# Gates spread from SBUF instead of DRAM, the inputs loaded first, a longer clear behind each scatter, and a new order of the streams

## The chip, the cores and the metric

The kernel runs on one core of a Trainium2 chip. The metric is the device time of one execution in microseconds (us). Beside the timed runs there is one execution with a profile; its span is the time from the first to the last recorded instruction.

## The reference

Eight sequences of 512 tokens with 128 features pass through four residual blocks. All arithmetic is float32.

```python
x = embeddings                                   # (8, 512, 128)
x = x + causal_attention(layernorm(x), W_Q, W_K, W_V)
x = x + moe_ffn(layernorm(x), Wg, W1, W2, W3, Ws1, Ws2, Ws3)
x = x + rwkv_block(layernorm(x), ...)            # scan over time, channel mix of width 512
x = x + moe_ffn(layernorm(x), Wg, W1, W2, W3, Ws1, Ws2, Ws3)
```

`moe_ffn` softmaxes `x @ Wg` over 32 experts and keeps the 4 largest per token. Each expert has a capacity of 2048 pairs of token and expert. A chosen expert gives `silu(x @ W1[e]) * (x @ W3[e]) @ W2[e]` (128 to 64 to 128 features), weighted with the softmax score, and a shared expert of width 128 is added.

## The kernel before

All eight sequences stay in SBUF as residual tiles `res0` to `res7` (128 x 4 x 128). Work is written as Python generators, one for each step of the network and each sequence or group; a `yield` ends a piece. `ORDER` is a long string of two-character names, and `play` takes one piece of the named stream at each. This sets the order of the instructions on every engine (PE, DVE, ACT, POOL) and of the DMAs that SP issues. [...]

The names in `ORDER`: `a` is attention with the routing of the first expert layer, `r` the RWKV block with the routing of the second, `x` and `y` the shared expert of the first and second layer. The expert layers are done in two ways, by sequence (`RUNS`):

- Paged (sequences 1 to 3 and 4 to 6 in layer one, 0 to 2 and 3 to 5 in layer two). `scatter` (`s` in layer one, `t` in layer two; L506) writes each normalized token row to four places of a DRAM buffer `xs`, sorted by expert. One sequence is 16 indirect DMAs, issued by POOL, with a `pause()` behind each: a memset of the tile `idle`, 128 x `PAUSE` columns (L308), which nothing reads. `experts` (`k l m n`, in layer two `K L M N`) loads 512 rows at a time (`xg<-xs`, L554), 20 units for a group of three sequences, and stores the results (`ys<-oc`, L616). The first unit of a group waits for all 48 scatters of the group. `combine` (`u`, `v`; L657) adds the rows back with 16 indirect DMAs for each sequence.
- Full (sequences 0 and 7 in layer one, 6 and 7 in layer two). Every expert is computed for every token, two experts at a time, in 16 steps. `gates` makes a tile `gT` with one row of gate values for each expert (32 x 512) and stores it to a DRAM tile `gd` (L495). `full_up` (`d`, `D`) spreads rows 2i and 2i+1 of `gd` to 64 partitions each: one DMA of 256 KB into a tile `g` (L692), three steps ahead, in four buffers. Each step has two matmuls (L703), a tanh on ACT (L706), and on DVE the products L709, L710 (which reads `g`) and L711. `full_down` (`e`, `E`) multiplies by W2 and sums (L677).

SP issues nearly all transfers in the order in which the pieces are played: gate loads, expert loads and stores are in one queue. The tiles of most intermediate results come from the pool `work`, `NWORK` buffers of one shape each. `gT` and the transposed input `fT` of a full sequence are such tiles; `fT` is held until the last step of `full_up`.

At the start SP issues the `x` tiles of sequences 0 to 3, then the clearing of `xs0` (two DMAs of 2600 KB, L182), then the tiles of sequences 4 to 7, then the expert weights `pair`, `w2s` and `w13s`. The weights of the other blocks (`sm`) come on ACT's queue.

Of the kernel before, what the change touches and what calls it, by code (L numbers as in the profile page):

```python
# [9 lines left out]
F32 = mybir.dt.float32  # L10
# [59 lines left out]
for _name, _w in (  # L70
# [9 lines left out]


ORDER = (
    "a2a0a2a1a0a2a2a0a1a3z0a2a0a1a6a3z0a0a2a3a4a2a0a1a0a6a6a4a1a2a2a5a0z0a0a2a2a1a4a5a0a0a2a5a2a0a0a2"
    "a1a3a0a3a2a7a2a0a2a0a2a1a2a2a0a3a7a0a2a1a6a3a0a0a7a2a0a2a1a2a1a0a2a1a2a2a3a0a2a1a4a3a1a2a2a0a0a1"
    "a2a0a0a3a2a0a5a1a2a2a3a2a0a0a1a1a3a2a1a1a3a0a1a2a0a7a3a0a2a0a1a2a0a3a2a0a1a3a2a6a1a0a3a1a6a0a3a6"
    "a2a1a0a3a6a2a2a0a1a0a3a2a6a2a2a0a1a6a6a0a1a3a0a1a1a0a3a0a1a6a0a1a1a0a0a3a6a3a3a1a1a3a0a6a6a1a0a0"
    "a3a1a6a2a1a3a0a6a2a3a6a4a3a4a3a4a1a1a3a4a4a1a0a5a4a4a5a1a1a3a0a6a3a1a0a3a1a6a1a4a6a3a4a4a1a3a6a1"
    "a5a3a6a3a4d0a6a5a1a3a3a6a1a1a3a2a1a4a2a5a4a4a5d0a2a1d0a5a5a2a5x0x0a2a1a2s1a3a3a6x2a4a5a6x2x0x2x2"
    "a5a6a3a4a3x2x2a6s2a4a4d0a3x2a6a3a4a6a5x0a3a4a6a5a4s2a3a6a4x0a6a3a3a4a5d0a3d0s2x0a3a6x0a7a3a6l0a6"
    "a4a7s3l0a6l0a6a4a5d0a4a5a4x3a6a4a6x3d0s3a4d0a4a5d0a7a5a5a7a5a7a4a5a7d0a6a4a5x3s3a6a4a5a4x3a5a4a5"  # L90
    "x3a4a5x3a4a5s3a5x3a5a5a7a5e0a7a5a7e0a7a5d0a4e0a5d0a7e0s2a5a6a4a5d0a5d0a6a7a6e0d0a6a7a5a7x1a5s1d0"
    "a7x1x1a4a7e0a7a4d0a4d0a4a7a4a7a7x1s1a4d0d0a7d0e0d0a7a4x1s1d0d0d0a4a4d0a7e0a4e0x1k0a5d0a6a4a5a6x1"
    "d0a5d0k0a4a5k0e0a5d0s4k0l0k0x4l0l0a5d0x4d0a5l0s4d0m0a5e0m0l0a5d0d0e0l0l0l0s4m0a5m0k0k0k0l0k0d0a5"
    "n0s4n0l0a5d0l0l0d0n0m0d0n0e0m0k0l0k0a7s5n0l0l0l0l0n0a6a7l0l0x4l0k0a6m0k0k0a6e0s5k0m0m0x5m0l0a6x5"
    "n0d0n0d0n0l0l0x5s5a6x5l0n0a7x4a7a6k0l1m0k0x5l1m0x5d0s6l1l0x5x4n0l0l0l0l0n0k0l0l0m0l0k0a7m0k0l0a7"
    "k0s6m0l0l0n0l0m0a7n0k0l0a7k0m0l0l0n0l0m0x4n0s6a7k0x4l0k0m0l0l0n0l0m0a7n0n0a7k0l0n0s6k0m0l0l0a7l0"
    "m0k0l0a7k0a7m0n0m0x6n0l0s5l0n0l0x6l0n0k0l0l0m0x6x6k0l0m0e0k0l0x6k0a7m0l0l0n0l0m0x6n0a7a7k0l0k0m0"
    "l0n0l0l0a7m0l0n0a7k0x6l0m0k0k0n0k0l0a7l0m0l0n0a7k0a7m0k0n0m0n0n0l0a7l0l0n0k1l0a7a7m0a7l0l0a7m0n0"
    "l0l0n0k1l0l0m0l0a7k1m0k1l1a7k1m0l1l1n0l1m0x7n0l1x7m1x7k1l1l1l1n0k1x7n0m1m1k1x7m1l1k1n1l1l1l1l1n1"
    "u2k1m1l1l1l1k1n1m1x7n1m1l1x7m1k1l1l1n1l1k1e7n1l1u2m1l1l1k1l1n1m1k1d0n1d0m1k1d0m1n1k1l1n1n1l1l1d7"  # L100
    "l1l1u2n1k1m1l1l1l1k1e0m1k1m1l1k1m1n1l1l1l1l1n1k1m1l1l1l1k1n1u2m1k1m1n1l1m1k1n1l1l1d0l1n1d0m1d0k1"
    "m1n1k1l1n1n1u1l1l1l1l1n1k1m1l1l1l1k1e0m1k1m1r2e0l1m1k1n1r0d7n1r2d7n1l1l1l1r0n1k1m1r2k1r0u1r0d7l1"
    "m1r0l1n1r0d7e7l1r0l1n1r2u1m1k1r0r0m1k1l1d7r0r0d7r0l1l1l1l1r0u1n1r0m1k1n1l1r2e7r2r0r2r0r0r0r0r0m1"
    "u3r0l1n1k1d7r0n1r0r2k1d7r2k1r0k1r2r0u3r0r0l1r0m1r1m1n1r0l1n1k1r1l1l1l1r0m1r1r0r1u3r2r2d7r1l1r1e7"
    "l1r0r1r0m1u3r0d7r0l1r1r0r2l1d7r1r0r2r2r2r2r0r1m1r0r0r1r1d7r0r0m1r3r1l1r0r0l1r1r3l1n1r0l1r0r1n1r3"
    "r1r1r3m1r0r0m1r1r1r1r2r1n1r0r2r3d7r0e7r0r1n1n1r1d7n1r0r0r1r0r1r0u4r0r0r1r1r0r1r0r1r2r0r1r0u4r0r0"
    "r1r2r1r0y0r1r3t0r2r1r3r2y0r1r1r3r2r3r1t0r2r1r3r1r1r3r3r2r1r1d7r3r2r1t0r3r1r3r2y0d7r1r2r1r3r3d7t0"
    "r3d7r3e7r1r1r3r3r2d7r1r2u4r3r2r1e7r2d7r3y0r2r2r2r3r2r2r1r2r2r3u4r2r2r1r2r2r3r3r1d7r3r1r3r2d7r1u5"
    "d7r1y0r2d7r1r4d7r1d7e7r4r1r2d7r3r2u5r1r4r4r1r4r1d7r2e7d7e7r4r4r1r3r2r3u5r1y1r4r4d7y1r3r4r4d7y1r3"
    "d7r3r4r2d7y1u5r4r3r4r4r4r4d7r3r4r3y1r4r4y1r3r4d7r3y1u6e7r4r3r4r3e7r3r3r4y0r3r4r3y0r5u6r4r4r2r2r3"  # L110
    "d7r3r4r4r5r2r3d7r2r3r4d7r2u6e7r5r2r5r4r2r5r2r5d7d7r4r5r3r2r2d7r2u6r4r5e7r5r4r4r2r4r5r5r5r2r4L0r3"
    "r3d7t2r4L0d7r4L0r6r5r4d7r3r5r4r4d7d7r5r6r4r4t2r3r6e7r5r5r4r4r5r5r5r5r6r5r3t2r6r5e7r4r3r4d7r5r5t2"
    "y2r4r4y2r5r5r6r3r4r6r5t1r4r5r6r6r4r3d7r6r6r4r3r3e7r4r5r4e7t1r4r6r5r5r4r5r6r5r6r4r3r6t1r4r3r5r5r6"
    "r5r4r5r5r5t1r4r5r5r5r5r5r5r6r4r4r6t4y4r5r6r5r6y4K0r6r6r5r5K0t4K0K0K0L0r6L0L0L0L0K0M0L0L0L0M0N0t4"
    "K0r6M0N0K0L0M0N0K0r6N0L0L0L0L0t4K0M0L0L0L0M0N0K0r6M0N0K0L0M0r3N0K0L0L0r7y3N0r5r6y3r5t3r5L0L0y3M0"
    "L0L0K0y4M0r5L0K0N0r5r6y2M0N0K0r6t3r5M0L0K0N0r5r5y3N0y4r5L0L0L0r6y3M0K0r5r5t3M0L0K0N0y3N0r5y2y3r7"
    "r5L0r6r5y5L0r6L0L0t5K0M0L0K0L1r7M0L1y4N0L0L1y2r7L0L0r6K0L0N0M0t5r6r7r7r6r6M0r7K0L0t5L0N0r6r7K0N0"
    "M0L0K0M0r6L0L0N0L0r6L0N0M0t5L0L0K0L0r6M0N0K0L0r6M0N0L0K0M0r6N0L0L0K0t3N0L0r6M0L0K0r6M0N0L0L0K0N0"
    "L0r6M0L0K0r6M0L0L0K0y5y5N0r6M0N0L0M0K0L0N0L0L0K0r6N0M0L0r6M0r6K0N0K0K0N0L0r6r7L0L0K0L0r7r6r7r6M0"
    "K0L0r7M0N0L0L0K0L0N0r6r7L0M0L0K1r7y5M0L0y4r6r7N0r7r7M0y4L0N0y5M0r6L0N0L0L0r6K1r7y5N0K1r6r7M0L1y5"  # L120
    "M0K1N0L1L1r6L1K1N0r7M1L1r6r6M1N1r6r7K1N1v0y2L1L1r6K1L1L1y2r6L1L1r7M1L1r6K1y6M1N1K1r7y6M1L1M1v2N1"
    "N1L1L1y6K1L1N1y6K1L1D6y6M1L1L1K1r7y6M1K1L1L1y6N1L1L1r7v2M1N1K1E6M1N1L1K1L1N1M1r7K1M1r7K1L1L1L1L1"
    "r7N1v2L1L1r7M1N1K1M1L1N1K1L1N1M1L1L1K1M1L1N1K1M1L1N1M1r7N1L1L1L1v2K1N1D6K1r7D6M1D6r7K1L1M1N1L1L1"
    "L1K1D6N1D6v0M1K1D6M1r7N1K1L1N1r7D6L1L1r7v2D6r7L1K1D6r7M1r7v0M1L1K1r7N1L1L1D6L1N1K1M1K1r7M1E6r7L1"
    "v0N1D6L1L1D6r7N1E6r7r7L1L1r7M1L1K1M1r7L1L1K1v1M1L1v0r7M1N1L1L1L1K1N1N1K1L1N1M1L1L1K1L1r7v1M1K1M1"
    "L1r7M1r7N1K1N1N1L1L1L1K1K1D6N1r7K1D6M1r7v1r7E6D6E6L1M1N1L1L1L1L1N1r7M1L1L1L1E6M1N1r7M1D6v1N1M1D6"
    "N1D6r7N1r7D6r7D6E6D6r7v4D6r7r7v1r7D6r7E6D6r7r7y7y7D6y7v4D6D6y7E6D6y7D6D6y7E6y7v4D6D6D6E7E6D6D6D6"
# [15 lines left out]
def kernel(ctx: ExitStack, tc: tile.TileContext, x, small, vecs, w13, w2, out):  # L143
    nc = tc.nc
# [8 lines left out]
    dram = ctx.enter_context(tc.tile_pool(name="dram", bufs=1, space=bass.MemoryType.DRAM))  # L153
# [44 lines left out]
    for s in range(2):  # L200
        for i in range(2):
# [3 lines left out]
                in_=w2[i * H : (i + 1) * H],  # L205
# [477 lines left out]
    def full_up(f, b):  # L683

        n = f"{f}_{b}"
        _, gd, xT, _ = routed[f][b]
        loaded = {}

        def load(i):
            if i < NP:  # L690
                loaded[i] = full.tile([P, S], F32, tag="g", name=f"g_{n}_{i}", bufs=4)
                nc.sync.dma_start(  # L692
                    out=loaded[i], in_=gd[2 * i : 2 * i + 2].unsqueeze(1).to_broadcast([2, H, S])
                )

        for i in range(3):
# [317 lines left out]
```

## Time and profile before

| what | value |
|---|---|
| median of the two timed runs | 1059.47 us (1058.66 to 1060.27) |
| the profiled execution | 1047.35 us |
| its span | 1045.6 us |
| mean granted clock of PE | 0.896 |
| gate loads `g<-gd` | 64, of 256 KB each |
| scatters `xs<-xn,rows`, mean | 192, of 1019 ns |
| pauses, memset 128 x 192, mean | 192, of 287 ns |
| combines `res<-ys,rows`, mean | 192, of 1610 ns |

Durations below are from the profiled execution. In the groups, a line gives the source line, the engine, the operation and the tiles, then busy us and mean ns of one, then the idle time of the engine ahead of the group and who ended it. In a line of the table of windows stand the window, the busy time of PE, of PE's weight loads, of DVE, ACT and POOL with their instructions, the granted PE clock, the busy share of the 16 DMA engines, and GB/s. The chain is followed back from the last instruction: each piece is what released the next one.

### The profile page before, as it was taken

What the parts mean: (1) busy time and instruction counts of PE and PEld (TensorE: products, weight loads), DVE (VectorE), ACT (ScalarE), POOL (GpSimd) and SP (SyncE); (2) the same over time, 40 slices, a digit from 0 to 9 for tenths busy, and PEclk for the clock granted to TensorE, in tenths of its full rate; (3) what the DMA queues carried; (4) which work ended last, traced back from release to release, by engine and by line L of the source; (5) the groups of instructions that cost most, each with busy time, mean ns of one, the idle gap of its engine ahead of it and who ended that gap; (6) DMA issues with size and microseconds to landing.
All of it is one profiled execution on the core that took longest, in us unless ns stands there. A gap on an engine that the chain in (4) does not pass through costs nothing.

```text
span 1045.6 us, 14396 instructions
## 1 busy us (share of the span) xinstructions
PE 806.6 (77%) x4096; PEld 559.8 (54%) x4096; DVE 588.2 (56%) x2008; ACT 474.1 (45%) x1130; POOL 617.1 (59%) x682
## 2 busy tenths in 40 slices
PE   4488689777599668787889888786993989856664
PEld 2266356555498555453455545564783757534332
DVE  2457576655245436699779679662482445522332
ACT  4375243323276447473445555455672656201010
POOL 4200778555701828848888888878036685788500
PEclk9699999978799979898999898898996999977787
DMA  9990112333356655322233211543456566344311
GB/s 271 249 262 25 69 57 74 110 91 100 94 143 160 137 136 126 58 56 33 59 59 54 41 42 42 158 114 107 111 138 129 126 147 137 80 75 91 65 58 54
DMA packets 158892, 108.15 MB, mean 103 GB/s; under 512 B 17760, under 2 KB 147168, under 8 KB 158560
## 3 DMA queue, kind: packets, MB, share of 16 engines
q1 hardware_dynamic: 124592, 80.59, 28.8%
q0 software_dynamic: 33792, 25.39, 13.9%
q10 hardware_dynamic: 432, 1.27, 0.4%
q8 instruction: 35, 0.57, 0.2%
q14 instruction: 41, 0.34, 0.1%
HBM read 60.32 MB, written 46.89 MB: 103 GB/s over the span
## 4 chain that ended last, share of the span: by engine, by line
PE 17%; DMA 13%; POOL 11%; issue 8%; DVE 7%; ACT 2%; SPq 1%; POOLq 0%; ACTq 0%; DVEq 0%
DMA g<-gd 7%; POOL res L657 6%; DMA xg<-xs 4%; POOL xs L506 3%; PE o L609 3%; PE acl L576 3%; PE turn_x L346 1%; DMA res<-ys,rows 1%; PE kk L926 1%; PE fsum L677 1%; PE ac L703 1%; POOL idle L308 1%; PE kv L935 1%; PE acl L597 1%; DMA ys<-oc 1%
## 5 line engine op out<-in xcount | busy, mean ns | idle before, releaser
L657 POOL DMA_INDIRECT res<-ys,rows x192 | 309.2, 1610 | 123.7 <-DMA xg<-xs 57.8
L506 POOL DMA_INDIRECT xs<-xn,rows x192 | 195.7, 1019 | 83.1 <-issue 61.8
L703 PE MATMUL ac<-fT,pair 128*128 128x512 f32 x256 | 138.9, 670 | 13.1 <-DVE g L710 13.0
L706 ACT ACTIVATE fh<-ac 128x512 f32<-128x512 f32 x64 | 38.2, 596 | 162.3 <-PE ac L703 130.6
L677 PE MATMUL fsum<-w2s,fh 128*128 128x128 f32 x512 | 78.5, 305 | 39.3 <-DVE fh L711 38.9
L677 PEld LDWEIGHTS fsum<-w2s,fh 128*128 128x128 f32 x512 | 73.1, 216 | 64.7 <-DVE fh L711 52.1
L576 PE MATMUL acl<-w13s,xgTs 128*128 x640 | 94.5, 294 | 16.3 <-issue 6.1
L609 PE MATMUL o<-w2s,hz 128*128 x640 | 94.1, 292 | 15.2 <-ACT wt L585 5.8
L609 PEld LDWEIGHTS o<-w2s,hz 128*128 128x128 f32 x640 | 85.4, 203 | 28.6 <-issue 11.6
L576 PEld LDWEIGHTS acl<-w13s,xgTs 128*128 128x128 f32 x640 | 85.0, 205 | 27.4 <-issue 13.4
L710 DVE TENSOR_TENSOR g<-g,ac 128x512 f32<-128x512 f32 x64 | 43.7, 682 | 88.7 <-DMA g<-gd 88.7
L346 PE MATMUL turn_x<-ident,xg 128*128 128x128 f32 x320 | 52.8, 292 | 46.7 <-DMA xg<-xs 45.5
L703 PEld LDWEIGHTS ac<-fT,pair 128*128 128x128 f32 x256 | 50.1, 215 | 59.6 <-issue 41.2
L564 ACT COPY xgTs<-turn_x 128x512 f32<-128x512 f32 x80 | 46.7, 583 | 72.5 <-PE turn_x L346 52.8
L335 POOL TENSOR_TENSOR rstd_f<-rstd_f,nhalf 128x4 f32<-128x4 f32 x16 | 19.5, 1217 | 100.6 <-DVE wt L581 42.6
L581 DVE TENSOR_TENSOR wt<-acl,xg 128x4 f32<-128x4 f32 x80 | 12.8, 161 | 108.9 <-PE acl L576 74.6
L587 DVE SCALAR_TENSOR_TENSOR h<-h,acl 128x256 f32<-128x256 f32 x80 | 33.5, 418 | 68.0 <-ACT h L584 59.0
L346 PEld LDWEIGHTS turn_x<-ident,xg 128*128 128x128 f32 x320 | 40.6, 152 | 52.9 <-DMA xg<-xs 39.5
L615 ACT COPY oc<-o 128x512 f32<-128x512 f32 x80 | 46.8, 585 | 41.5 <-PE o L609 20.9
L602 ACT COPY hz<-acl 64x256 f32<-64x256 f32 x160 | 58.2, 364 | 13.2 <-PE acl L597 8.5
L709 DVE SCALAR_TENSOR_TENSOR fh<-fh,ac 128x512 f32<-128x512 f32 x64 | 43.6, 681 | 26.3 <-ACT fh L706 17.3
L308 POOL MEMSET idle<- 128x192 f32 x192 | 55.0, 287 | 0.0
(265 smaller groups left out, 1615.0 us busy)
## 6 DMA issues: line engine op xcount, KB each, us to landing
xg<-xs SPq DMA_DIRECT2D x80, 260.0 KB
ys<-oc SPq DMA_DIRECT2D x80, 256.0 KB
g<-gd SPq DMA_DIRECT2D x64, 256.0 KB
xs<-zero SPq DMA_DIRECT2D x4, 2600.0 KB
xs<-xn,rows POOLq DMA_INDIRECT x192
res<-ys,rows POOLq DMA_INDIRECT x192
res<-in_x_dram SPq DMA_DIRECT2D x8, 256.0 KB
pair<-in_w_dram SPq DMA_DIRECT2D x1, 2048.0 KB
```

Source lines behind the costliest of these rows:

```text
L308: nc.gpsimd.memset(idle, 0.0)
L346: nc.tensor.transpose(p[:, j * P : (j + 1) * P], src[:, j, :P], ident)
L506: i = nc.gpsimd.indirect_dma_start(out=xs[g][:, :], out_offset=bass.IndirectOffsetOnAxis(ap=rows[:, j, k : k + 1], axis=0), in_=xn[:, j, : ...
L564: nc.scalar.copy(xT, p)
L576: nc.tensor.matmul(acl[:, j, :EW], xT[:, j * P : (j + 1) * P], w13f[:, bass.ds(at[j], EW)], start=True, stop=True)
L602: nc.scalar.copy(z[half, i, :].rearrange("p (j c) -> p j c", c=H), hT[half])
L609: nc.tensor.matmul(o[:, j * P : (j + 1) * P], z[:, j % 2, j // 2 * P : (j // 2 + 1) * P], w2h[j % 2][:, bass.ds(at[j], P)], start=True, st ...
L615: nc.scalar.copy(flat(oc), o)
L657: nc.gpsimd.indirect_dma_start(out=xa[:, j, :], out_offset=None, in_=ys[g][:, :], in_offset=bass.IndirectOffsetOnAxis(ap=rows[:, j, k : k ...
L677: nc.tensor.matmul(p[:, j * P : (j + 1) * P], h[:, j * P : (j + 1) * P], w, start=False, stop=stop and j == NJ - 1)
L703: nc.tensor.matmul(ac[:, s, :], pair[:, i, s, :], xT, start=True, stop=True)
L710: nc.vector.tensor_tensor(v, v, ac[:, 1, :], ALU.mult)
```

## The change

There are four edits. `gd` is gone: `gT` stays in SBUF and each gate load reads its two rows from there. All eight `x` tiles are issued ahead of the clearing of `xs0`. The tile that a pause clears has 640 columns instead of 192, and `work` has 25 buffers instead of 26. `ORDER` is a new string of the same 2257 pieces; within a stream they keep their order, but they stand differently against other streams' pieces. In SP's queue, for example, 14 gate loads of sequence 0 stand ahead of the first expert load of layer one (12 before); `g_7_0` to `g_7_3` stand ahead of the first expert load of its second group (before, three gate loads stood ahead of the eleventh); and in layer two four gate loads stand ahead of the second group's eleventh expert load (before, three ahead of the eighth).

```diff
-PAUSE = 192
-NWORK = 26
+PAUSE = 640
+NWORK = 25
...
 ORDER = (
-    "a2a0a2a1a0a2a2a0a1a3z0a2a0a1a6a3z0a0a2a3a4a2a0a1a0a6a6a4a1a2a2a5a0z0a0a2a2a1a4a5a0a0a2a5a2a0a0a2"
+    "a1a2a2a0a1a2a2a1a0a3z0a2a1a0a6a3z0a1a2a3a4a2a1a0a1a6a6a4a0a2a2a5a1z0a1a2a2a0a4a5a1a1a2a5a2a1a1a2"
...
-    load_x(0, 4)
+    load_x(0, B)
...
     clear(0)
-    load_x(4, B)
...
         gT = block([E, S], name=f"gT_{n}")
         nc.scalar.copy(gT, p[:E, :])
-        gd = dram.tile([E, S], F32, tag=f"gd{n}", name=f"gd_{n}")
-        nc.sync.dma_start(out=gd, in_=gT)
-        routed[f][b] = (xa, gd, xT, None)
+        routed[f][b] = (xa, gT, xT, None)
...
-        _, gd, xT, _ = routed[f][b]
+        _, gT, xT, _ = routed[f][b]
...
                 nc.sync.dma_start(
-                    out=loaded[i], in_=gd[2 * i : 2 * i + 2].unsqueeze(1).to_broadcast([2, H, S])
+                    out=loaded[i], in_=gT[2 * i : 2 * i + 2].unsqueeze(1).to_broadcast([2, H, S])
                 )
```

More of the change, by code (lines that the diff above doesn't have):

```diff
@@ L82 @@
 ORDER = (
-    "a2a0a2a1a0a2a2a0a1a3z0a2a0a1a6a3z0a0a2a3a4a2a0a1a0a6a6a4a1a2a2a5a0z0a0a2a2a1a4a5a0a0a2a5a2a0a0a2"
[L84 to L127, printed above, removed]
@@ L128 @@
-    "E6v4D6D6D6D6D6E6D6D6D6D6D6v3E6D7E6D6D6E6v4D7D7D7E6v3E6D7D7D7E7D7D7D7E7v3D7D7D7E7D7D7v3D7E7D7D7D7"
-    "E7D7v5D7D7E7v3D7D7D7E7v5D7D7D7E7D7D7D7E7v5D7D7D7E7D7D7D7E7v5D7D7D7D7D7E7D7D7D7D7D7E7E7v5D7D7E7E7"
+    "a1a2a2a0a1a2a2a1a0a3z0a2a1a0a6a3z0a1a2a3a4a2a1a0a1a6a6a4a0a2a2a5a1z0a1a2a2a0a4a5a1a1a2a5a2a1a1a2"
+    "a0a3a1a3a2a7a2a1a2a1a2a0a2a2a1a3a7a1a2a0a6a3a1a1a7a2a1a2a0a2a0a1a2a0a2a2a3a1a2a0a4a3a0a2a2a1a1a0"
+    "a2a1a1a3a2a1a5a0a2a2a3a2a1a1a0a0a3a2a0a0a3a1a0a2a1a7a3a1a2a1a0a2a1a3a2a1a0a3a2a6a0a1a3a0a6a1a3a6"
@@ new lines @@
+    "a2a0a1a3a6a2a2a1a0a1a3a2a6a2a2a1a0a6a6a1a0a3a1a0a0a1a3a1a0a6a1a0a0a1a1a3a6a3a3a0a0a3a3a6a0a3a6a0"
+    "a6a0a3a6a0a3a6a0a3a4a3a4a4a0a3a3a6a4a0a0a6a3a4a6a3a0a6a0a3a0a3a3a4a0a0a6a4a6a6a4a3a0a3a3a6a6a0a1"
+    "a0a2a3a6a0a3a2a4a5a1a6a1a2a5a3a2a1a3a6a3a6a6a2a1a3a5a5a1a5a2a5s1a5a7a5a5a7a7a2a0a7a2a0a3a0x2d0d0"
+    "s2x2a6x2d0a3a4a4a5a5d0x2a3a6a3a4d0a4d0a4s2a3a5a5a5a3x2a3x2l0a6x2a4s3l0a6a5a4l0a5a4a6x3a6a5a6a4a5"
+    "d0x3a4a5a4a4a5a6a6a5d0s3d0a4a4a5a5a4x0a4a5a4x0x3a4a5d0a4a5x3a5a4a4a6x3a5a4s3d0a6a4a5x0a4a5a4a4a5"
@@ new lines @@
+    "a4a5x3a4s3a5x3x0a5a7x0a5a7a5x0a5a7x0x1a7a7a4x1e0a7a4a5a7e0x1a6a7a5s2x1e0x1a6d0x1a6d0a7a6x1a7d0a7"
+    "d0d0a7e0s2e0d0a7d0d0a7e0a7a7a7d0a7d0d0a7s1e0a4d0a7a4d0e0a4d0a4a7a4a7a7a4d0s1d0a7a4d0a7d0a4a4d0a7"
+    "e0a4s1e0a6d0a4a6d0d0e0a4x4d0s4x4k0a5x4x4d0x4a7x4d0d0a7k0x4a5k0k0l0a5s4k0a5l0l0d0l0a5d0k0a5m0k0a7"
+    "e0m0l0a7d0n0a5n0l0s4l0l0k0a5l0a5k0m0a6m0l0l0l0l0a6a5k0m0k0e0s4m0n0d0n0l0l0a6a5n0d0a7n0l0e0k0m0a6"
+    "k0m0n0l0n0a6a5x5l0l0l0s5x5k0x5m0k0x5m0a6l1l0x5x5d0l0l0l1l0l0x5n0s6l0l0l0m0n0e0m0k0l1k0m0k0a7l0m0"
@@ new lines @@
+    "a7k0n0d0l0l0l0n0d0k0d0m0k0n0s6m0x6n0l0x6n0x6l0l0l0l0n0k0l0l0m0l0k0x6m0e0x6k0l0k0s6m0l0l0n0l0m0x6"
+    "n0k0x6l0k0m0l0l0n0l0m0l0n0s6k0l0l0m0l0n0k0m0k0l0n0k0m0l0l0n0l0m0l0n0k0l0l0m0l0n0k0a7m0k0s5l0n0a7"
+    "k0m0a7l0n0a7l0l0m0l0n0a7k0l0l0m0l0n0k0k0m0s5a7k0l0n0m0a7k0l0l0a7m0n0k0d0n0l0d0n0m0n0d0m0l0s5a7l0"
+    "l0l0l0a7a7m0a7l0l0n0a7m0e0l0n0n0e0a7n0r0m0a7x7m0d7d7x7r0d7x7n0k1r0x7r0d7r0k1r0x7d7r0k1n0d7d7k1r0"
+    "r0k1l1r0r0u2r0l1l1l1k1r0m1r0l1m1r0n1l1r0r0d7k1r0r0r0x7l1u2r0n1d7x7r0e7r0e7e7r0r0u2r0r0l1r0k1m1d7"
@@ new lines @@
+    "k1m1l1r0n1u2d7n1l1l1l1d7e7k1m1d7k1m1l1n1l1l1l1l1n1k1r0m1l1l1l1k1e7m1u1k1m1r0r0l1r2n1m1r0l1r0d7r0"
+    "k1l1r0n1l1d7r2k1r0d7m1r0m1n1u1r0r0r2k1l1r0r0l1l1d7r0l1r0r2m1k1e7m1u1r0l1r0k1l1l1l1n1d7d7m1k1m1l1"
+    "r0k1u1r0l1l1l1m1r0k1l1r0k1r2n1l1r2e7r0l1r2l1n1u3m1m1r0r0k1r1l1n1k1l1r0l1l1r0r0r2k1n1m1m1r2r0r1r0"
+    "k1l1r2u3r0l1l1r1l1r1k1r2r2r0r0k1r1r0r2n1u3n1n1m1m1r1r2l1r0r0r1r2n1m1l1l1n1l1r1l1r2k1n1l1m1l1r2r1"
+    "t0m1l1k1l1r2r1m1k1r1r2l1l1r1r2k1l1n1r1y0n1r2m1m1k1t0l1k1r1y0n1l1l1r2r1n1n1l1m1l1r1r2n1m1k1m1n1k1"
@@ new lines @@
+    "l1r2d7l1t0n1d7k1l1n1k1k1r1n1m1m1n1l1r2r1n1k1n1l1l1l1r1t0n1m1r2m1r2r1l1r2r1n1l1l1l1n1m1r1u3m1r2n1"
+    "l1n1r1l1l1l1m1r1m1n1r2r1n1r3r3r2r2r1r1u4d7r2r1r3d7r3r2r1e7y0r3r3y0r2r2y0r1d7y0r1u4r2d7r1r3y0r2r3"
+    "r3r2r2r3r3r3r2u4r1r3r3r2r1d7r3r1r3r2r1r3d7r3r2d7r3u4e7r1r2r1r3r2r1r3r3r3r1d7r3r1u5r1d7r3e7r1r1r4"
+    "r1r1r3r2r4r3d7u5r2r4r3r1r4r3r4r1r4r2r4r2r3r1u5r3r3r1d7e7r4r4d7d7r3r4r4r4r3r3r3r2r4r4r1r4d7u5r4r4"
+    "r3r3r4r2r4r4e7r3r3r4r3r3r4r2r4u6r2r3r4r3r3r3r4r2d7r4r4r5u6r2r4r2r3r3r4r2r3r1r1r3r4r1d7r5r1r1r4r3"
@@ new lines @@
+    "r1r4r5d7r1u6e7r5r4r3r1r4r4r3r4r1r1r5u6r4r5r1r4r5d7r4r4r1d7r5r5r4r1r4r5r5t1y1r4r4r6y1r5r4y1r4r5r5"
+    "r5r5r5r5r6r5r5y1r4t1r4y1r5r5y1r4r5r2r4y1r4r5r3r2d7r3t1r4d7r5r3e7r3r5r5r2r5r5t1r2r2r3r5r2y2y2L0L0"
+    "r5t2r5r3r6L0d7r4r5d7r5y2r4r5r5r3r4r6r3r4t2e7r4r5r5d7r4r6r5r3r4r3r6d7r5t2r4r6r5r4r5r6r6r5r4r5r6d7"
+    "r5r3t2r4r5d7r4r6d7y3r5r5y3y3t4y3r5K0r5r6y3y3r6r6r6K0y3y4K0K0r6r6L0t4K0r6e7L0L0e7L0r6L0y4e7M0r6K0"
+    "M0y2K0N0L0r6L0N0L0L0t4K0M0L0L0L0M0N0K0r6M0N0K0L0r6M0N0K0L0L0r6N0L0L0r5K0L0L0t4M0L0M0N0K0r5M0r5r6"
@@ new lines @@
+    "L0K0M0L0r6N0N0L0L0K0N0L0M0r7t3K0M0r5K0N0r5L0L0y4r5N0L0L0r5K0M0L0L0r5r6M0K0N0L0r6r7L0N0M0r6K0t3M0"
+    "r5K0L0L0r7L0r7N0L0y2N0M0L0L0K0L0r7y4r7y4r6y4M0r6t3K0M0r5r5N0r6L0r5M0K0N0N0K0r6y4r7N0L0L0r6L0L0t3"
+    "r5r7M0r5K0M0L1r7L0L0r6K0N0L0r7L1N0L0L1r7M0K0M0L0r6L0L0K0t5N0r6M0N0L0M0K0L0N0L0L0K0r6N0L0r6M0L0K0"
+    "M0r6L0N0t5L0K0L0N0r6M0L0K0r6M0r7L0L0K0r6N0M0r7r7L0M0N0N0t5L0L0K0N0L0r6K0K0L0r6M0L0L0r6M0L0K0r7r7"
+    "r7t5M0r7N0r6M0L0N0N0r7r7L0L0K0r7N0r6K0L0r7M0L0r6r7M0y5N0L0L0L0K1y5y2N0r6M0y2M0r6y5y5K1N0y5K1r6L1"
@@ new lines @@
+    "r6r7K1y5L1N0r7L1K1r6y5L1L1r6K1M1L1L1L1K1r6v0M1K1M1r6r7L1K1M1N1L1L1r6r7N1L1L1r7K1M1L1L1L1K1N1v0M1"
+    "K1M1N1r6r7M1K1L1r6r6N1r6L1L1r6N1N1L1L1N1K1v0M1L1L1L1K1r6M1K1M1r6L1M1D6K1N1L1L1D6L1N1D6K1M1K1N1D6"
+    "M1v0y6N1L1y6N1y6L1L1L1L1N1K1M1L1L1L1K1y6M1K1M1y6L1K1M1N1r7L1L1L1L1N1v1K1M1L1L1L1K1N1v0M1y6N1r7r7"
+    "M1L1M1K1L1N1L1L1K1D6v1N1D6M1K1D6y6M1N1L1K1N1D6L1L1L1D6N1D6M1K1N1r7M1L1v1K1r7N1L1L1D6r7N1L1r7M1K1"
+    "r7r7M1K1N1v1r7L1N1r7L1L1E6L1r7r7K1r7M1r7M1E6L1K1D6N1v2L1L1D6r7r7N1L1v1M1L1r7M1K1L1L1N1L1K1v2L1N1"
@@ L130 @@
+    "M1L1L1K1L1r7M1K1M1L1r7M1r7K1D6K1v2L1L1L1N1E6N1M1D6N1M1D6E6N1L1N1L1L1L1D6N1D6r7M1D6v2E6M1N1E6N1r7"
+    "D6r7r7D6E6D6r7r7r7D6r7v4D6E6D6r7v2D6r7r7r7D6r7E6D6r7v4r7y7y7D6y7D6D6y7E6D6y7D6v4D6y7E6y7E7D6D6D6"
+    "E6v4D6D6D6D6D6E6D6D6D6D6D6v5E6D7E6D6D6E6v4D7D7D7E6v5E6D7D7D7E7D7D7D7E7v5D7D7D7E7D7D7v5D7E7D7D7D7"
+    "E7D7v3D7D7E7v5D7D7D7E7D7v3D7D7E7D7D7D7E7v3D7D7D7E7D7D7D7E7v3D7D7D7D7D7E7D7D7D7D7E7D7D7E7D7v3E7E7"
     "E7"
```

## The prediction, made before the changed kernel ran

> **What bounds the kernel now.** I read the page first: no engine is busy over 77% of the span, so no single engine is the bound, and its chain and groups name what to look at.
>
> ```profile
> PE 806.6 (77%) x4096; PEld 559.8 (54%) x4096; DVE 588.2 (56%) x2008; ACT 474.1 (45%) x1130; POOL 617.1 (59%) x682
> ...
> DMA g<-gd 7%; POOL res L657 6%; DMA xg<-xs 4%; POOL xs L506 3%; PE o L609 3%; PE acl L576 3%; PE turn_x L346 1%; DMA res<-ys,rows 1%; PE kk L926 1%; PE fsum L677 1%; PE ac L703 1%; POOL idle L308 1%; PE kv L935 1%; PE acl L597 1%; DMA ys<-oc 1%
> ...
> L710 DVE TENSOR_TENSOR g<-g,ac 128x512 f32<-128x512 f32 x64 | 43.7, 682 | 88.7 <-DMA g<-gd 88.7
> L308 POOL MEMSET idle<- 128x192 f32 x192 | 55.0, 287 | 0.0
> ```
>
> The change touches four entries: gate loads (`g<-gd`), scatters (`xs` L506), pauses (`idle`), and expert loads (`xg<-xs`). The chain in order of time (start, length, what) puts all of `g` in the last 90 us, and some `xg` around 790 to 860:
>
> ```profile
> 790.98 18.30 DMA xg<-xs
> ...
> 832.86 11.78 DMA xg<-xs
> ...
> 852.99 10.70 DMA xg<-xs
> ...
> 958.40 17.41 DMA g<-gd
> ...
> 978.93 37.70 DMA g<-gd x2
> ...
> 1018.24 19.78 DMA g<-gd
> ```
>
> The timeline of DVE shows the step of this tail: one product with a gate tile at 994.60, 999.96, 1005.29, every 5.35 us, each after a wait. The table of windows gives the DMA there:
>
> ```profile
> 992.00:1010.00 18.00, 11.73 (x40) 6.25 (x38) 5.93 (x9) 2.12 (x4) 0.00 (x0) 0.91 0.18 63
> 1010.00:1040.00 30.00, 16.30 (x58) 9.46 (x59) 11.26 (x17) 2.66 (x5) 0.00 (x0) 0.83 0.15 54
> ```
>
> The last column but one is the busy share of 16 DMA engines: 0.15 to 0.18, little over 2/16. So a 256 KB gate load runs on two engines, 64 packets of 2 KB each, 5.35 us = 64 x 84 ns (the packet records show 84 to 87 ns). While POOL's combines run beside it (912 to 990), the step is 7.0 us (11 intervals in 77.0). From 912.24 to 1038.04 there are 20 intervals, all set by gate loads. At 790.98 the `xg` load follows three gate loads in SP's queue: 3 x 5.35 = 16 us, and PE's timeline shows it waiting 16.95 us there.
>
> Two more waits, one of the DMA queue, one of DVE (by form: for whom, us, times, longest), and the rate of a POOL memset:
>
> ```profile
> SPq L554 <- DMA xs<-xn,rows: 80.3, 2, 78.1
> ...
> DVE stats_a L314 <- DMA res<-in_x_dram: 24.9, 2, 16.9
> ...
> L276 POOL MEMSET hz<- 128x512 f32 x3 | 1.5, 524 | 0.0
> ```
>
> The 78.1 us end at 653: the first expert group of layer two can't load before its 48 scatters, and POOL is 180 of 219 us busy from 434 to 653. The 16.9 us end at 32.80: the fifth `x` tile lies behind the clearing of `xs`.
>
> **What the skill says.** DMA: Bandwidth & Descriptors, "Why a DMA increments its semaphore by 16 and not by 1": a transfer uses the largest number of engines up to 16 that divides the slowest dimension of both sides. The gate's source has 2 rows, so 2; the trace agrees (above). Same page, "Queues, rings and completion order": an engine takes descriptors of one ring in order; the 16.95 us wait agrees. SBUF — State Buffer, "Door 1: The DMA port swizzle": four neighbouring partitions share one port, and a transfer over partitions 0 to 3 measured 27.6 GB/s. The trace agrees on writes: the `w2s` loads to 64 partitions (8 ports) ran at 182 GB/s with 53 ns for 512 B, the `x` tiles to 128 partitions at 356 GB/s with 27 ns. On reads it speaks twice. The first `gd<-gT` store, alone in the queues, reads 32 partitions (8 ports) by 16 engines: median 144 ns for 2 KB instead of 84. The three later ones, behind other traffic, show mostly 84 to 96 ns; they could have been read ahead. So sharing is likely on reads, not certain.
>
> **Part 1, gates from SBUF.** Rows 2i and 2i+1 of `gT` are neighbouring partitions: both engines now read through one port. Bounds for a load: 5.35 us (no sharing) and 11.5 us (256 KB at 182/8 = 22.8 GB/s, the `w2s` rate per port). I take 9.5 us, the page's 27.6 GB/s, an estimate; 64 x 144 ns gives 9.2. Going away: four `gd` stores of 64 KB and 1.2 us of SP's wait; 1 us, set at nothing.
> Tail: steps of `d` at 828 to 876 (five) are paced by PE's order. Loads 8 to 31 come after: 24 x 9.5 = 228 us from 876.5 is 1104.5, where the last product stood at 1038.0: +66. The combines' packets on the same two engines cost 1.65 us a load now (7.0 - 5.35); one engine can use the port while the other serves them, so I add 0.7 x 13 = 9. Tail +75.
> Second expert group of layer two: in the new order four gate loads stand ahead of its eleventh `xg` load (three ahead of the eighth before): 38 us against 16, less one step more of other work, and three later gate loads at +4.2 between `xg` loads, half of it seen: about +20.
> Layer one: `g_7_0` to `g_7_3` now stand ahead of the very first `xg` of the second group, 38 us, with some 18 us of PE work in between: +20, of which half dies in POOL's own backlog before 653: +10. Before, no gate load stood there. First group: its first `xg` goes out behind 14 gate loads, 12 before. Loads were issued 7.9 us apart; at 9.5 some two are outstanding: +19, less what part 3 gives.
>
> **Part 2, pauses of 640.** 524 ns at 512 columns and 287 at 192 make 0.74 to 0.84 ns a column: 640 take 632 ns, +345 each, 66 us of POOL in all. A scatter's pitch is 1.41 us now, so 1.76. On the path: the 48 before the first `xg` of each layer, 48 x 0.345 = 17 us each. The other 96 are covered: layer one's second group has three gaps of 10 to 11 us, layer two's ends at 729.8, 20 us ahead of POOL's next work. If that cover is gone, 17 us more.
>
> **Part 3, `x` first.** The first four tiles are there at 9.54; four more at 356 GB/s make 3 us, so all have landed by about 13. The 16.9 us wait goes; next is the power on POOL for tile 6, behind the weights' work there until 21.5, now at 34.3: -11. The clears end later, but the first scatter is at 107.8.
> First group of layer one together: scatters -11 + 17 = +6, the ring +19 from a first issue near 195; first landing about 214 where it was 196: +18.
>
> **Part 4, a work tile fewer, and `gT` in one of them.** No row shows a wait for a work tile. Bounds: 0 (the order is new and was free to avoid it) and about 20 us (one such wait of a chain's length); I take 0. The rest of the new order: -15 to +15, taken as 0.
>
> **Sum.** 18 + 10 + 17 + 20 + 75 = +140. The profiled execution took 1047.35 us (span 1045.6): 1187. The median of the two timed runs, 1059.47, lies 12.1 above it, so 1199.
>
> **Rivals.** A, the forecast: shared port, 1199; its own range 1150 to 1260 (loads of 9.2 to 11.5 us, slack of 30). Chance 0.64.
> B: reads don't share the port (the three later stores speak for it). A load stays 5.35; left are -11, 17 + 17, and about +2 from the loads ahead of `xg`: +25, so 1084; with slack less. Chance 0.20, split over the bound: 0.12 same, 0.08 slower.
> C, the other side: loads at 5.35 us, and the new place of the first gate loads takes the 18.3 us `xg` wait off the path, while PE (191 of 219 us busy from 434 to 653) hides the longer scatters. Then -11 - 18 + 6 = -23: 1036. It decides if a gate packet takes 84 ns and no `xg` wait over 5 us is left. Chance 0.09: 0.06 faster, 0.03 same.
> D: A and also waits for work tiles or loads of 11.5 us throughout: 140 + 20 + 24 x 2 + 20 is 1287. Chance 0.07.
> That the change doesn't do what it says: the memsets are 640 wide and the loads read `gT`; only a spread over more engines could differ, which two source rows exclude.
>
> Range: 1055 takes in B, 1260 the top of A; left out are C, D and the ends of A, about 0.2. About 2% can be told from no change. Faster 0.07, same 0.16, slower 0.77 (A 0.62, B 0.08, D 0.07); of A's 0.64, 0.01 each is left to same and faster, should the new order save more than I can see.
>
> **What would show it.** Right: steps of about 9.5 us between products with gate tiles in the tail, 2 KB packets near 145 ns, DVE's idle time ahead of the gate product two to three times 88.7; memsets of 632 ns, scatters 1.76 us apart; no wait of DVE for `x` over 5 us. Wrong: gate packets at 84 ns and steps of 5.35, then B or C; or a tail that starts much earlier than 876, so that loads of 9.5 us are spread over work.

## The result and the profile after

The changed kernel takes 1249.05 us (median of two runs, 1247.2 to 1250.89), 1.1789 times the kernel before [1.1705, 1.1874]. The forecast was 1199. The profiled execution took 1247.20 with a span of 1245.5: +200 on the one before, where the sum said +140.

First the page of the changed kernel: busy time by engine, the chain by line, and four groups (busy us, mean ns of one, then the idle time ahead and who ended it).

```profile
span 1245.5 us, 14382 instructions
PE 850.1 (68%) x4096; PEld 585.9 (47%) x4096; DVE 596.5 (48%) x2008; ACT 473.7 (38%) x1130; POOL 688.7 (55%) x682
...
DMA g<-gT 27%; DMA xg<-xs 7%; POOL xs L503 6%; POOL res L654 6%; POOL idle L307 4%; PE acl L573 2%; PE o L606 2%; PE ac L700 1%; DMA xs<-xn,rows 1%; SPq L613 1%; PE turn_x L345 1%; PE s L756 1%; PE o L776 1%; PE kk L923 1%; SPq L551 1%
L654 POOL DMA_INDIRECT res<-ys,rows x192 | 305.1, 1589 | 224.9 <-DMA res<-ys,rows 104.5
L707 DVE TENSOR_TENSOR g<-g,ac 128x512 f32<-128x512 f32 x64 | 43.8, 684 | 245.8 <-DMA g<-gT 245.8
L307 POOL MEMSET idle<- 128x640 f32 x192 | 125.8, 655 | 0.0
```

Gate loads went from 7% to 27% of the chain, and DVE's idle time ahead of the gate product from 88.7 to 245.8 us, 2.8 times. The products themselves cost what they did (684 ns). A memset takes 655 ns where 632 were estimated. The combines (L654) wait 104.5 us for the landing of earlier combines, 1.9 in the kernel before, and the forecast has no such wait.

The chain in order of time (start, length, what) shows that gate loads are not its tail alone:

```profile
138.96 47.80 DMA g<-gT x2
186.75 27.42 issue
...
367.70 25.70 DMA xg<-xs
...
933.04 40.48 DMA xg<-xs x3
...
994.40 243.23 DMA g<-gT x9
```

DVE's timeline in the tail has the step between two gate products; each waits for its load:

```profile
1057.35 0.69 DVE L707 TENSOR_TENSOR g<-g,ac 128x512 f32<-128x512 f32 x1 [9.01 <-DMA g<-gT]
1068.11 0.69 DVE L707 TENSOR_TENSOR g<-g,ac 128x512 f32<-128x512 f32 x1 [8.74 <-DMA g<-gT]
1077.42 0.69 DVE L707 TENSOR_TENSOR g<-g,ac 128x512 f32<-128x512 f32 x1 [7.30 <-DMA g<-gT]
```

From 1004.29 to 1237.65 there are 23 such intervals, 10.15 us each on average. The twelve beside POOL's last combines (up to 1134.64) take 10.86 us each, where the step beside combines was 7.0; the eleven behind them take 9.36, where the undisturbed step was 5.35. The packet records agree: 2 KB packets have a median of 153 ns over the run, 165 in the first 230 us and 155 after 1000, where it was 84. The table of windows (PE, weight loads, DVE, ACT and POOL busy, granted clock, DMA share, GB/s) shows that this is not a full DMA system: the share is still about 2/16, and the bytes moved fell from 63 and 54 GB/s to

```profile
1110.00:1230.00 120.00, 60.30 (x144) 32.56 (x144) 23.41 (x37) 7.16 (x12) 12.43 (x8) 0.67 0.17 36
```

So about two engines are busy, as before (0.17 of 16 here), and move some 60% of what they did. The granted clock of PE in this window is 0.67, where it was 0.91 and 0.83; DVE waits for a gate load in these steps, so PE's pace does not set them.

The loads act early too. SP's timeline has the first fourteen gate loads, then PE's has two transpositions of expert tiles, the first of layer one and the first of its second group, with the wait ahead of each:

```profile
96.87 132.44 SPq L689 DMA_DIRECT2D g<-gT  x14
...
255.42 1.12 PE L345 MATMUL turn_x<-ident,xg 128*128 128x128 f32 x4 [28.50 <-DMA xg<-xs]
...
393.54 1.09 PE L345 MATMUL turn_x<-ident,xg 128*128 128x128 f32 x4 [40.26 <-DMA xg<-xs]
```

Fourteen loads in 132.44 us are 10.2 us apart over 13 intervals. The first transposition stood at 196.24 before. POOL's timeline shows that the scatters of the second group were late as well. The first line is the last of the first group's 48 scatters, the second the next one, the first of sequence 4; POOL found nothing to do for 27.61 us between them:

```profile
185.14 0.97 POOL L503 DMA_INDIRECT xs<-xn,rows  x1 [0.16 <-issue]
...
214.37 0.97 POOL L503 DMA_INDIRECT xs<-xn,rows  x1 [27.61 <-issue]
```

Between two scatters that follow one another the pitch is 1.79 us (183.35 to 185.14). Part 3 did what was said: the longest wait of DVE for `x`, 16.9 us before, is 4.2, and the first scatter starts at 90.97 where it was 107.8.

```profile
DVE stats_a L313 <- DMA res<-in_x_dram: 6.3, 2, 4.2
```

### The profile page after: what moved, and what is told of

Its sections match the earlier page's. It is cut to its first block, busy times and chain, and to the rows that moved or that the text cites. A ratio compares the mean times of both kernels' runs of the same rounds, so it can differ in the third digit from the quotient of the medians.

```text
span 1245.5 us, 14382 instructions
## 1 busy us (share of the span) xinstructions
PE 850.1 (68%) x4096; PEld 585.9 (47%) x4096; DVE 596.5 (48%) x2008; ACT 473.7 (38%) x1130; POOL 688.7 (55%) x682
## 4 chain that ended last, share of the span: by engine, by line
DMA 35%; POOL 18%; PE 18%; issue 16%; DVE 6%; ACT 4%; SPq 2%; POOLq 0%; ACTq 0%; DVEq 0%
DMA g<-gT 27%; DMA xg<-xs 7%; POOL xs L503 6%; POOL res L654 6%; POOL idle L307 4%; PE acl L573 2%; PE o L606 2%; PE ac L700 1%; DMA xs<-xn,rows 1%; SPq L613 1%; PE turn_x L345 1%; PE s L756 1%; PE o L776 1%; PE kk L923 1%; SPq L551 1%
## 5 line engine op out<-in xcount | busy, mean ns | idle before, releaser
L654 POOL DMA_INDIRECT res<-ys,rows x192 | 305.1, 1589 | 224.9 <-DMA res<-ys,rows 104.5
L503 POOL DMA_INDIRECT xs<-xn,rows x192 | 201.0, 1047 | 124.2 <-issue 64.7
L700 PE MATMUL ac<-fT,pair 128*128 128x512 f32 x256 | 158.6, 753 | 28.6 <-DVE g L707 28.3
L707 DVE TENSOR_TENSOR g<-g,ac 128x512 f32<-128x512 f32 x64 | 43.8, 684 | 245.8 <-DMA g<-gT 245.8
L674 PE MATMUL fsum<-w2s,fh 128*128 128x128 f32 x512 | 87.3, 327 | 93.3 <-DVE fh L708 93.3
L674 PEld LDWEIGHTS fsum<-w2s,fh 128*128 128x128 f32 x512 | 81.2, 237 | 125.8 <-DVE fh L708 111.1
L307 POOL MEMSET idle<- 128x640 f32 x192 | 125.8, 655 | 0.0
L573 PE MATMUL acl<-w13s,xgTs 128*128 x640 | 98.3, 301 | 18.5 <-ACT hz L599 10.0
L573 PEld LDWEIGHTS acl<-w13s,xgTs 128*128 128x128 f32 x640 | 88.4, 212 | 29.3 <-ACT hz L599 13.1
L700 PEld LDWEIGHTS ac<-fT,pair 128*128 128x128 f32 x256 | 57.7, 246 | 84.1 <-issue 50.2
```

The lines of the kernel that those rows point to most:

```text
L307: nc.gpsimd.memset(idle, 0.0)
L503: i = nc.gpsimd.indirect_dma_start(out=xs[g][:, :], out_offset=bass.IndirectOffsetOnAxis(ap=rows[:, j, k : k + 1], axis=0), in_=xn[:, j, : ...
L573: nc.tensor.matmul(acl[:, j, :EW], xT[:, j * P : (j + 1) * P], w13f[:, bass.ds(at[j], EW)], start=True, stop=True)
L654: nc.gpsimd.indirect_dma_start(out=xa[:, j, :], out_offset=None, in_=ys[g][:, :], in_offset=bass.IndirectOffsetOnAxis(ap=rows[:, j, k : k ...
L674: nc.tensor.matmul(p[:, j * P : (j + 1) * P], h[:, j * P : (j + 1) * P], w, start=False, stop=stop and j == NJ - 1)
L700: nc.tensor.matmul(ac[:, s, :], pair[:, i, s, :], xT, start=True, stop=True)
```

## The experiments

The variants ran on three chips, with the kernel before beside them on each: it took 995.87 us beside e1 to e4, 995.12 beside e5 to e8 and 1044.76 beside e9 to e12. Every ratio is to the kernel before on the same chip. What was expected of e1 and e2 in microseconds starts from the 1059 us of the first runs and is to be read as a difference: e1 is within it (+9 where +1 to +36 was expected), e2 somewhat dearer (+207 where +141 to +191 was expected).

**Which property of the gate loads costs the time.** Three kernels: the change with gates from DRAM, the old kernel with gates from SBUF, and the change with gates from SBUF but rows i and i + 16.

```diff
 # e1_gates_dram: the changed kernel, and
-        routed[f][b] = (xa, gT, xT, None)
+        gd = dram.tile([E, S], F32, tag=f"gd{n}", name=f"gd_{n}")
+        nc.sync.dma_start(out=gd, in_=gT)
+        routed[f][b] = (xa, gd, xT, None)
 # e2_only_sbuf: the kernel before, with the reverse of this edit
 # e3_rows_apart: the changed kernel, with the two experts of a load put 16 rows apart in gT
-        nc.vector.tensor_tensor(gate, gate, ex, ALU.mult)
+        apart = rt.tile([P, NJ, E], F32, tag="adr", name=f"apart_{n}")
+        nc.vector.tensor_tensor(
+            apart.rearrange("p j (s n) -> p j n s", s=2), gate.rearrange("p j (n s) -> p j n s", s=2),
+            ex.rearrange("p j (n s) -> p j n s", s=2), ALU.mult,
+        )
...
-            nc.tensor.transpose(p[:E, j * P : (j + 1) * P], gate[:, j, :], ident)
+            nc.tensor.transpose(p[:E, j * P : (j + 1) * P], apart[:, j, :], ident)
...
-                    out=loaded[i], in_=gT[2 * i : 2 * i + 2].unsqueeze(1).to_broadcast([2, H, S])
+                    out=loaded[i], in_=gT[i : E : NP].unsqueeze(1).to_broadcast([2, H, S])
```

> The changed kernel with the gates stored to DRAM and spread from there as before; everything else as changed. If the source of the gates carries the change: 2 KB packets back at 84 ns, steps of 5.35 us in the tail, and 1060 to 1095 us (what is left is +34 for the pauses ahead of the first expert loads, -11 for the start, and the new order). If the pauses and the new order carry it: 1150 us or more.

> The kernel before with one edit alone: gate loads read their rows from gT in SBUF. If the source carries the change: 1200 to 1250 us, gate steps of 10 to 10.6 us in the tail. If it needs the new order or the pauses: under 1120 us.

> The changed kernel, still spreading from SBUF, but the two rows of a load lie 16 partitions apart (rows i and i+16 of gT, permuted when the gates are made), so that by the skill's port map they have different ports. Theory of the shared port: packets at 84 ns, steps near 5.35 us, the time of the run with gates from DRAM within 20 us. Rival, an SBUF source is slow whatever its partitions: packets stay near 150 to 165 ns and the time near 1249 us.

| kernel | us | ratio to before | 2 KB packet, median |
|---|---|---|---|
| e1_gates_dram | 1004.76 | 1.0090 [1.0064, 1.0115] | 84 ns |
| e2_only_sbuf | 1203.27 | 1.2082 [1.1992, 1.2173] | 153 ns |
| e3_rows_apart | 999.32 | 1.0029 [1.0009, 1.0050] | 84 ns |

The group of gate products on the page of each, e1, e2 and e3 in this order:

```profile
L709 DVE TENSOR_TENSOR g<-g,ac 128x512 f32<-128x512 f32 x64 | 43.7, 683 | 101.5 <-DMA g<-gd 101.5
```

```profile
L708 DVE TENSOR_TENSOR g<-g,ac 128x512 f32<-128x512 f32 x64 | 43.7, 684 | 185.7 <-DMA g<-gT 185.7
```

```profile
L711 DVE TENSOR_TENSOR g<-g,ac 128x512 f32<-128x512 f32 x64 | 43.7, 683 | 94.0 <-DMA g<-gT 94.0
```

The last one settles it. e3 reads its gates from SBUF, as the change does, in the same order of the streams and with the same pauses; only the two rows of a load no longer lie next to each other. Its steps in the tail are again 5.35 us:

```profile
943.93 0.69 DVE L711 TENSOR_TENSOR g<-g,ac 128x512 f32<-128x512 f32 x1 [3.34 <-DMA g<-gT]
949.27 0.69 DVE L711 TENSOR_TENSOR g<-g,ac 128x512 f32<-128x512 f32 x1 [2.54 <-DMA g<-gT]
```

SBUF as a source costs nothing here (e3 against e1). Two engines that read neighbouring partitions do, which fits what the Trainium skill says of ports ("SBUF — State Buffer", section "Door 1: The DMA port swizzle"): four neighbouring partitions share one. 256 KB in the 9.36 us of a step without combines are 28.0 GB/s, near the 27.6 that the page has for a transfer over partitions 0 to 3. Only rows 1 and 16 apart were tried; that the thing shared is this port rests on the page and on that rate. Alone, in the old order, the SBUF rows cost 207 us (e2), and in the new one 245 to 250 (the change against e1 and e3).

**The pauses and the `x` tiles.**

```diff
 # e4_pause_192: the changed kernel, and
-PAUSE = 640
+PAUSE = 192
 # e6_before_pause640: the kernel before, with the reverse
 # e7_before_x_first: the kernel before, and
-    load_x(0, 4)
+    load_x(0, B)
...
     clear(0)
-    load_x(4, B)
```

> The changed kernel with pauses of 192 columns. My step of 17 us on the path in each layer: 1215 to 1235 us. If the longer pauses are covered, as PE and the gate loads are late anyway: 1245 to 1250 us.

> The changed kernel unaltered, to stand on the same chip as its variants: in the first measurement 1249 us against 1059 (1.179). If the gate loads set its time, it is near 1240 to 1250 us on any chip, whatever the kernel before takes there, and lies 15 to 35 us over the variant with pauses of 192; if those are covered, within 10 us of it.

> The kernel before with pauses of 640 columns alone (work tiles and order as before). My step: +34 us (17 in each layer, ahead of the first expert loads). If PE and DVE, which are 80% busy there, hide them: under +10 us. If POOL is also late for the second groups: +66 us.

> The kernel before with all x tiles loaded ahead of the clears, alone. My step: -11 us, as DVE's wait of 16.9 us goes. If the time comes back at the next wait: -3 to 0 us.

e4 took 1231.34 us (1.2360 [1.2279, 1.2441]), and e5, the changed kernel unaltered, 1249.64 (1.2554 [1.2464, 1.2645]). Their kernels before agree to 0.8 us, so inside the change the longer pauses cost some 18 us, half of the 34 forecast: the natural reading, not tested further, is that the rest lies beside waits for gates. In the kernel before they cost 52 (e6: 1047.57, 1.0514 [1.0459, 1.0570]), more than the 34. In e6's trace the first transpositions of the four groups stand 28, 36, 50 and 58 us later than in e7's, whose earlier `x` tiles make 14 of each: so the second groups, whose pauses the forecast took as covered, lose 8 us each as well. The `x` tiles first bring 15 us (e7: 980.42, 0.9827 [0.9769, 0.9884]) where 11 were forecast.

**The new order, and the kernel before against itself.**

```diff
 # e10_new_order_only: the kernel before with the ORDER of the change and
-NWORK = 26
+NWORK = 25
```

> The kernel before unaltered: its median was 1059 us in the first measurement and 995 us beside the variants, and there is no trace of the shorter one. If the chip's TensorE clock makes it, PE's rows are shorter all through and the gate steps stay 5.35 us; if it is one wait, one stage alone is shorter by some 60 us.

> The changed kernel's order of the streams and its 25 work tiles alone: gates from DRAM, pauses of 192, x tiles loaded in two parts as before. I had put this at 0, between -15 and +15 us of the kernel before. If the order was fitted to slower gates and pauses it loses 10 us or more without them; if it is better by itself, -20 us or more.

e9 took 1044.86 us, 0.9989 [0.9963, 1.0015] of its like: on this chip the kernel before is long again, so e9 does not show how it comes to 995 elsewhere. e10 took 1052.85: 1.0054 [1.0019, 1.0089]. The order with one work tile fewer costs 6 us or so: taken as 0 in the forecast, within its -15 to +15.

**More engines for a gate load.** If two engines are the limit, a source with more rows should lift it. Here each row of `gd` is stored eight times, so a load has 16 rows of source.

```diff
 # e8_before_16_engines: the kernel before, and
-        gd = dram.tile([E, S], F32, tag=f"gd{n}", name=f"gd_{n}")
-        nc.sync.dma_start(out=gd, in_=gT)
+        gd = dram.tile([E, 8, S], F32, tag=f"gd{n}", name=f"gd_{n}")
+        nc.sync.dma_start(out=gd, in_=gT.unsqueeze(1).to_broadcast([E, 8, S]))
...
-                    out=loaded[i], in_=gd[2 * i : 2 * i + 2].unsqueeze(1).to_broadcast([2, H, S])
+                    out=loaded[i], in_=gd[2 * i : 2 * i + 2].rearrange("e c s -> (e c) s").unsqueeze(1).to_broadcast([16, H // 8, S])
 # e11_16_engines_x_first: this and the x tiles first;  e12_and_pause_8: also PAUSE = 8
```

> The kernel before, but gT is stored to DRAM in 8 copies of each row, so that a gate load has 16 source rows and runs on 16 engines instead of 2. If two engines set the pace of the tail: steps fall from 5.35 us to what PE, ACT and DVE need, 3.5 to 4.5 us, the expert loads no longer wait behind gate loads, and 40 to 70 us go. If the combines or the DMA as a whole set it: 0 to 15 us.

> The kernel before with gates from 8 copies in DRAM on 16 engines, and all x tiles first. If the two gains are in different stages they add: 889 less 15, so 870 to 880 us. If the start's gain was only passed through a stage that no longer sets the end: 885 to 890.

> The same, with pauses of 8 columns (about 98 ns each instead of 287). If the pause is pure time on POOL: half of what 640 added, reversed (52 us x 189/345 = 28 us), so about 845 to 855. If the scatters behind each other then wait for something else (descriptors, the DMA queue): scatters longer than 1.0 us and no gain, or a loss.

e8 took 888.58 us, 0.8909 [0.8855, 0.8963], 107 us less than its kernel before and more than expected. Its steps in the tail fall to 2.7 us (810.25 to 845.75, 13 steps), where 3.5 to 4.5 were expected. The packet records show that the loads are spread: while 2 KB packets move, two are under way at once for 77% of the time in the kernel before, and here the number is spread, with 16 the commonest (13%). On its page PE is busy 86% of the span, the chain has no gate load left, and the wait ahead of the gate products is 7.7 us where it was 88.7:

```profile
PE 759.4 (86%) x4096; PEld 533.7 (60%) x4096; DVE 589.2 (66%) x2008; ACT 474.7 (54%) x1130; POOL 620.8 (70%) x682
...
POOL res L657 19%; POOL xs L506 7%; PE o L609 3%; PE acl L576 3%; POOL idle L308 2%; DMA res<-ys,rows 2%; DMA xg<-xs 1%; PE turn_x L346 1%; PE ac L703 1%; POOL rstd_p L816 1%; PE kk L926 1%; PE acl L597 1%; PE k L800 0%; PE kv L935 0%; PE k
...
L710 DVE TENSOR_TENSOR g<-g,ac 128x512 f32<-128x512 f32 x64 | 43.5, 680 | 7.7 <-DMA g<-gd 7.7
```

e11 took 925.73, 0.883 [0.876, 0.890] of the kernel before on its chip, the lowest ratio of the study; its interval overlaps e8's, so what the `x` tiles add here is not told apart. It beats both kernels of this case. e12, with pauses of 8 columns, missed: 983.59, 0.9383 [0.9312, 0.9455], 58 us slower than e11 where 28 were to be saved. A pause took 132 ns on average, not 98. Its scatters take as long as e11's (0.97 us each) and follow one another every 1.28 us, but the other engines stall beside them. In the list of waits much of that has no releaser in the record ("remote" is what the list puts there; the chain on e12's page calls it "another core or an unknown queue", 9%). The longest such entries of e12, of e11 and of the kernel before (engine, line, us in total, times, longest):

```profile
DVE wt L580 <- remote: 35.8, 5, 11.5
ACT xgTs L563 <- remote: 18.9, 4, 7.8
DVE res L783 <- remote: 16.4, 2, 9.2
```

```profile
ACT fh L705 <- remote: 15.6, 3, 5.8
DVE wt L580 <- remote: 12.0, 3, 6.5
```

```profile
DVE wt L581 <- remote: 12.7, 4, 5.9
```

All such waits in the list together are 140.5 us in e12, 55.5 in e11, 49.0 in the profile of the kernel before. They are mostly waits of ACT and DVE for tiles that PE makes, and they fall in stretches with scatters. What holds PE's results back stays open: no run separates a cause.

## Why the prediction was right, and where its sum was not

The mechanism was right in its main links: two engines on neighbouring partitions, 153 to 165 ns for 2 KB, steps of nearly twice 5.35 us, expert loads late behind gate loads, pauses partly on the path, the wait for `x` gone. Rivals B and C needed 84 ns in the changed kernel and fall with its 153; e3 shows why, as it has the 84 ns when the rows are apart. D counted waits for work tiles or loads of 11.5 us: e3, which also has 25 tiles and `gT` in them, is within 4 us of the kernel before, and the loads took 10.2 on average.

The sum of +140 was short of +200. e3 shows where, since it runs the same pieces in the same order and differs in the place of the rows alone. The table has the moment of each event in us; the last column is what the forecast's sum holds for gate loads, added up (12, 10, 20, 75). The 12 are the first group's 18 less 6 for pauses and `x`: of its +19 in the queue, 7 had been there before.

| event | e3 | changed kernel | later by | forecast for gates |
|---|---|---|---|---|
| first expert transposition, layer one | 197.23 | 255.42 | 58 | 12 |
| first of layer one's second group | 311.39 | 393.54 | 82 | 22 |
| first of layer two | 625.42 | 751.04 | 126 | 22 |
| last expert load issued | 817.2 | 973.0 | 156 | 42 |
| end | 995.2 | 1245.5 | 250 | 117 |

**"Layer one, first group: +19" failed as a step.** It took the loads to be issued 7.9 us apart and two of them outstanding. SP's timeline of e3 has the fourteen loads 6.7 us apart:

```profile
100.69 87.14 SPq L693 DMA_DIRECT2D g<-gT  x14
```

At 10.2 us apart they take 45 us more (132.44 less 87.14): the delay adds up over the fourteen, not over the last two. The first expert load is issued at 229.40 (189.64 in e3), and PE has its tile 26 us later (8 in e3). The 48 scatters of this group are not what was late: they end at 186.11, and at 184.57 in e3.

The steps also hold up what is played between them, the routing of sequence 4. DVE ends a routing (L464) at 213.43, behind gate products that waited for their loads, and the first scatter of sequence 4 follows at 214.37; in e3 it starts at 190.30, after a wait of 5.08 us in place of 27.61. POOL's 384 scatters and combines come in one and the same order in both kernels, however long one of them waits.

**"Second group of layer one: +10".** The four gate loads ahead of its first expert load were seen, but were to be half hidden in POOL's backlog. The transposition waits 40.26 us in the changed kernel and 19.90 in e3, and the group is another 24 us later (58 to 82): no half of it was hidden.

**From there to layer two's first group** the forecast has no gate cost, and 44 us came. One wait there is in none of its steps: combines wait for earlier combines to land, 37.6 us in all between 393 and 751, where e3 has 2.3 in its like stretch (310 to 625). Over the whole run the lists of waits have, the changed kernel first and then e3:

```profile
POOL res L654 <- DMA res<-ys,rows: 104.5, 41, 6.9
```

```profile
POOL res L658 <- DMA res<-ys,rows: 9.2, 17, 1.0
```

The forecast knew that combines and gate loads share engines, but priced it one way, as 0.7 us on a gate load. The other way round was dearer. POOL sets the end of this stretch, as its last scatter is done 5 us ahead of the transposition. It is busy equally long in both kernels (265 and 266 us) and idle for 92 us against 48, and 35 of these 44 us are the waits. POOL's lag behind e3 grows from 87 to 126 us while it issues combines, and stays there over the scatters that follow. e2, with neighbouring rows in the old order, has 94.7 us of such waits. So they come with the slow gate loads; that the packets of the two queue behind each other on shared engines is argued, not shown.

**"Second group of layer two: +20"** gave 30 (126 to 156): the chain stands on expert loads from 933 to 973.

**"Tail: +75"** gave 94. The price of a load was right (9.36 us without combines, 9.5 forecast); beside combines a step cost 1.5 us more, 0.7 forecast. For the last 23 loads that makes 233 us, where 23 of 9.5 and 9 for the combines, 228, were counted. What was off besides is the first of the 24. It was counted as 9.5 us from the fifth of layer two's 32 gate products, but its own product, the ninth, waits for no load: it stands 18.6 us behind the fifth here (985.68 to 1004.29) and in e3, and 21.3 in the kernel before, whose timeline shows it:

```profile
876.46 0.68 DVE L710 TENSOR_TENSOR g<-g,ac 128x512 f32<-128x512 f32 x1
...
897.78 0.68 DVE L710 TENSOR_TENSOR g<-g,ac 128x512 f32<-128x512 f32 x1
```

**Parts 2 to 4** were forecast at -11 + 17 + 17 + 0 = +23. With the gates' cost taken out they come to +3 (e3) to +9 us (e1). Taken singly they are 52 for the pauses, -15 for `x` and 6 for the order, 43 in all: they don't add up, and longer pauses cost less in the changed kernel than in the one before.

The gates thus cost twice the 117 us forecast on the chips of e1 to e8. **That 1199 still stands only 50 below the measured 1249 is in part luck.** The kernel before took 1059 us in the runs of the forecast and 995 on those chips, while the changed kernel took 1249 in both places. Set against 995 the ratio is 1.2554, against 1059 it is 1.1789; from 995 the same +140 would have given 1135, 114 short.

The profile of the kernel before holds 49.0 us of the waits with no recorded releaser and so does e9 (48.4, at 1045 us); the changed kernel has none in either place, and none of the profiles of e1 to e8 has any. The 49 us are about the 50 by which the same kernel differs between chips. They also stand where the time goes: beside e7, which had the `x` tiles first but none of these waits, e9's groups are 16, 42, 41 and 56 us later, so it loses time from the first group to the second and from the third to the fourth, where most of its waits lie (212 to 281 and 671 to 727). The count goes with the pauses where such waits occur at all (140.5 us at 8 columns, 42 to 56 at 192), and the changed kernel with 640 columns had none in the runs of the forecast, where the kernel before had them. That longer pauses suppress them there would explain both ratios; the slower gate loads could do it too. Neither is shown: the record does not say if both kernels ran on one chip there, and no kernel with 640 columns and DRAM gates ran on a chip with such waits.

## What to carry to other kernels

Before rows are taken from SBUF instead of DRAM, look at which partitions a transfer reads at once: with two neighbours a load took nearly twice as long, and one stride in the layout (rows 16 apart) made 250 us here. A transfer on two engines is worth spreading first, by a source with more outermost rows; it brought 11%. And when a load gets slower than the step that uses it, price it for every stretch in which steps stand ahead of other work in an engine's order, not just for the tail: 156 of the 250 us lost here came before the last expert load.

## What was not expected of the hardware

- The kernel before took 1059 us in the runs of the forecast, and 995, 995 and 1045 on the three chips of the variants, up to 6% apart, while its runs on one chip agree within 1.5%. The longer times go with some 49 us of waits, mostly of ACT and DVE for PE's results, to which the record gives no releaser.
- Shorter pauses between scatters made the kernel slower on one of those chips: 8 columns instead of 192 cost 58 us although each scatter kept its 0.97 us, and longer ones (640) cost 52 us on a chip without such waits. Each of these chips had two widths, in different kernels; 192 was the better one on both.
- One memset of 128 x 640 takes 655 ns, a little over the 632 that the rates of two shorter ones gave.
- A first store, `gd<-gT`, alone in the queues, had shown 144 ns for 2 KB and later ones 84 to 96; long loads show 153 to 165. The later ones were no evidence against a shared port: a store of 64 KB behind other traffic doesn't show what 64 packets on two engines do.
